# Moving the first attention's stores to ScalarE's queue, and the transposes of a feed-forward layer from TensorE to VectorE and DMA

## The chip, the cores and the metric

The kernel runs on one core of a Trainium2 chip. TensorE (PE) multiplies matrices and does transposes as a multiplication with the identity; VectorE (DVE), ScalarE (ACT) and GpSimd (POOL) work on rows; SyncE (SP) only issues DMAs here, and ACT and POOL can issue DMAs as well. Each engine works through its own instructions in order, and waits on semaphores for the others. The metric is the device time of one execution in microseconds, as a median over runs.

## The reference

A block of four layers on an input of 4 batches of 512 rows and 512 columns, in float32:

```python
x = x + attn_a(layernorm(x))   # 16 query heads, 4 key/value heads, of 128 columns
x = x + ffn(layernorm(x))      # 512 -> 1408 -> 512
x = x + attn_b(layernorm(x))   # 16 heads, weights in 4 bits with scales per block of 32
x = x + ffn(layernorm(x))      # the same weights as above
```

What the change touches is in `attn_a` and in the last `ffn`. `attn_a` is the mean of two attentions on the same projections:

```python
y     = softmax(causal(rotary(q) @ rotary(k).T * D ** -0.5)) @ v
# gated linear attention: a running state per head, with a decay per key column
S     = S * exp(logsigmoid(k) / 16) + softmax(k) outer v
o_gla = softmax(q) @ S
attn_a = (0.5 * y + 0.5 * o_gla) @ Wo
```

The feed-forward layer quantises its weights to -1, 0 and 1, and is `(sigmoid(x @ w1.T) * (x @ w2.T)) @ w3.T`.

## The kernel before

The work lies on partitions in chunks of 128 rows; a batch has 4 chunks. `bank` gives a PSUM bank. The four layers run one after another, with some preparation of each next one inside.

**First attention.** One group is a key/value head (index g) with its four query heads, on one batch (b): 16 groups, 64 chunks. `step(n)` does a piece of work for each of six neighbouring chunks, called u, v, w, x, y and z for chunks n-2 to n+3, so a chunk passes through six steps. Per chunk these pieces are:

- `A` (z): the query projection by `wq`, four query heads side by side, to `q_t`.
- `B` (z): softmax of the queries times the decay (`qd`), for the linear attention; DVE transposes it in blocks of 32 by 32 (`turned`, L461), the result is stored to DRAM (`queries`, L463, on SP, 256 KB); the rotary embedding gives `qr`, with POOL doing the products `sw` (L345).
- `L` (y, in the next step): four DMAs fetch `queries` back to `qdT` (L470), so that blocks come to stand transposed. A transpose of 128 by 128 is thus the 32 by 32 blocks by DVE and the order of the blocks by DMA.
- `C` (y): PE transposes `qr` to `qrT`.
- `D(0)` to `D(3)` (x), one for each head: scores against the group's keys up to this chunk (L490, between 128 and 512 columns), negated row maximum by DVE (L494), exponential by ACT (L497), reciprocal (DVE, L498), division by the sum on ACT (L499), transpose in blocks by DVE into `turned` (L500). After the fourth head, `D` stores `turned` as `passed` (L503, on SP, 256 KB for the first chunk of a group to 1 MB for the fourth).
- `E` (w, in the next step): four DMAs fetch `passed` back to `prT` (L509).
- `own` (w): the linear attention's scores inside the chunk (L480, from `kdT` and `qdT`), masked by DVE to `own_` (L482).
- `F` (v, a step later): POOL adds `own_` to the part of `prT` on the diagonal (L515), then PE multiplies with the state (L518) and with the values (L520), and ACT halves it into `oT` (L522).
- `G` (u): the output projection by `wo` and the residual.

`part` works on a group ahead: keys and values (`project`), `gates`, `decays` (the cumulated decays `down` and the softmax of the keys times their inverse, `kd`; the decays at the ends of three chunks are copied across partitions by three small DMAs, `ends`, L420, on SP), `transposes` and `states`. ACT issues the loads of `wq` (L386) and `wo` (L390).

`step(n)` runs for n from -7 to 65. For n from 0 to 63 PE's instructions keep the order in which they are written (`manual_schedule`). Elsewhere a scheduler orders each engine's instructions by its own estimate of times; what is wrapped in `in_place` keeps its place in the written order. The DMAs of both stores and both fetches are `in_place`. Two more jobs run inside the steps: quantising the feed-forward weights (`quant`), and the layer norm of a batch to come (`ln`).

A DMA signals its end on one of eight completion semaphores, which are dealt in turn to the DMAs of SP and ACT together; so each of these DMAs waits for the one eight issues before it.

**Feed-forward layer.** `feed_forward` loads the 22 weight blocks (`block`, L264, on SP), keeps them, and goes through the 4 batches. Per batch there are 11 blocks f: 16 matmuls (`sc`) of two weight slices with the normalised input `xn`, which is kept as two halves (`hi` rounded to a faster format, `lo` the rest), a sigmoid on ACT (L1097), the product on DVE (L1098) and its halves (`split`, L120 on ACT and L121 on DVE). Then 4 output projections of 22 matmuls, the residual (L1109) and, in the last layer, the store of the result (L1111). The halves of the next batch are made inside this loop by `halved`, in steps driven by `next(steps, None)`: DVE normalises a chunk (`xn`, L160), PE transposes it in four 128 by 128 transposes (`tp`, L165), ACT and DVE split it. The halves of batch 0 are made before the layer begins.

`project` (L188) issues the matmuls of all projections. The DMAs of the whole program: 2035 on SP, 41 on ACT, 96 on POOL.

Of the kernel before, what the change touches and what calls it, by code (L numbers as in the profile page):

```python
# [9 lines left out]
F32 = mybir.dt.float32  # L10
# [3 lines left out]
F32R = mybir.dt.float32r  # L14
AF = mybir.ActivationFunctionType
ALU = mybir.AluOpType
# [3 lines left out]
P = 128  # L20
B, S, C = 4, 512, 512
NC = S // P
NK = C // P
# [51 lines left out]
def hybrid_block(ctx: ExitStack, tc: tile.TileContext, a: dict, out: bass.AP):  # L75
# [44 lines left out]
        nc.scalar.copy(hi, src)  # L120
        engine.tensor_tensor(lo, src, hi, ALU.subtract)  # L121

    def layernorm_steps(b, sink, tag="tp", apart=False, place=lambda i: i):

        mv = lnp.tile([P, NC, 2], F32, tag="mv", name="mv")
        rstd = lnp.tile([P, NC], F32, tag="rstd", name="rstd")

        def moments(c):  # L130
            st = lnp.tile([P, 6], F32, tag="st", name="st")
            nc.vector.bn_stats(st, xs[b * NC + c])
            nc.vector.bn_aggr(mv[:, c, :], st)

        def scales(at):

            var = lnp.tile([P, NC], F32, tag="var", name="var")[:, at]
# [7 lines left out]
            nc.vector.tensor_tensor(r, r, t, ALU.mult)  # L145

        if not apart:
            for c in range(NC):
                moments(c)
                if c == 1:  # L150
                    yield
            scales(slice(0, NC))
        for c in range(NC):
            if apart:
                moments(c)
                scales(slice(c, c + 1))
            else:
                yield
            xn = lnp.tile([P, C], F32, tag="xn", name="xn", bufs=1)
            nc.vector.tensor_scalar(xn, xs[b * NC + c], mv[:, c, 0:1], rstd[:, c : c + 1], ALU.subtract, ALU.mult)  # L160
            if not apart:
                yield
            tp = bank(tag, [P, NK, P])
            for k in range(NK):
                t = nc.tensor.transpose(tp[:, k, :], xn[:, k * P : (k + 1) * P], ident)  # L165
                if k == 0:
                    place(t)
            sink(c, tp)
# [5 lines left out]
    def halved(pool, b, **kw):  # L174

        halves = [pool.tile([P, NK, S], F32R, tag=f"xn{n}", name=f"xn{n}") for n in ("hi", "lo")]
        return halves, layernorm_steps(b, lambda c, tp: split(*(h[:, :, c * P : (c + 1) * P] for h in halves), tp), **kw)

    def whole(pool, b):

# [130 lines left out]
    def first_attention_gentle(base, extra):  # L311
# [6 lines left out]
        with ExitStack() as st:  # L318
# [55 lines left out]
            class Group:  # L374
# [32 lines left out]
                def decays(self):  # L407

                    dec = bank("mm", [P, NC, D])
                    halves = [one.tile([P, NC, D], F32R, tag=tag, name=f"gate{x}") for x, tag in (("hi", "held"), ("lo", "kd"))]  # L410
                    split(*halves, self.gate)
                    project(dec.rearrange("p c d -> p (c d)"), lambda i: until, lambda i: halves[i].rearrange("p c d -> p (c d)"), 2)

                    held = one.tile([P, NC, D], F32, tag="held", name="held")
                    nc.vector.tensor_scalar(held, dec, -2.0 * GENTLE * GATE_NORM, None, ALU.max)
                    self.down = two.tile([P, NC, D], F32, tag="down", name="down")
                    nc.scalar.activation(self.down, held, AF.Exp, scale=1.0 / GATE_NORM)
                    self.ends = two.tile([P, NC - 1], F32, tag="ends", name="ends")
                    for c in range(NC - 1):
                        nc.sync.dma_start(self.ends[:, c : c + 1], self.down[P - 1 : P, c, :])  # L420
# [24 lines left out]
            class Chunk:  # L445
# [9 lines left out]
                def B(self):  # L455
                    c = self.c
                    qd = one.tile([P, HG, D], F32, tag="qd", name="qd")
                    softmax_decayed(qd, self.q_t, lambda h: self.k.down[:, c, :])

                    turned = one.tile([P, 4, HG, 32], F32, tag="turned", name="turned")  # L460
                    nc.vector.transpose(turned.rearrange("p q h t -> p h q t"), qd.rearrange("p h (q j) -> p h q j", q=4))  # L461
                    self.queries = dram.tile([P, HG * D], F32, tag="queries", name="queries", bufs=3)
                    in_place(nc.sync.dma_start(self.queries, turned.rearrange("p q h t -> p (q h t)")))  # L463
                    self.qr = two.tile([P, HG, D], F32, tag="qr", name="qr")
                    rotate(self.qr, self.q_t, turn[:, c : c + 1, 0:1, :], turn[:, c : c + 1, 1:3, :])

                def L(self):
                    qdT = two.tile([P, 4, HG, 32], F32, tag="qdT", name="qdT", bufs=4)
# [15 lines left out]
                def D(self, h):  # L484

                    c, n = self.c, self.c + 1
                    if h == 0:
                        self.turned = late.tile([P, HG * P * (3 + c % 2)], F32, tag=f"turned{c % 2}", name="turned")[:, : 4 * HG * 32 * n]
                    sc = bank("sc", [P, 4, 32 * n])
                    nc.tensor.matmul(sc.rearrange("p q (k j) -> p q k j", j=32), lhsT=self.qrT[:, h, :], rhs=self.k.krT.rearrange("p (k q j) -> p q k j", q=4, j=32)[:, :, :n, :], start=True, stop=True)  # L490
                    nm = two.tile([P, 1], F32, tag="nm", name="nm", bufs=4)
                    flat = sc.rearrange("p q x -> p (q x)")

                    nc.vector.tensor_tensor_reduce(sc, sc, causal[:, :, 32 * (3 - c) :], -1.0, 3e38, ALU.add, ALU.min, nm)  # L494
                    pr = two.tile([P, S], F32, tag="pr", name="pr", bufs=5)[:, : P * n]
# [3 lines left out]
                    nc.scalar.mul(pr, pr, den)  # L499
                    nc.vector.transpose(self.turned.rearrange("p (q h x) -> p q h x", q=4, h=HG)[:, :, h, :], pr.rearrange("p (q x) -> p q x", q=4))  # L500
                    if h == HG - 1:
                        self.passed = dram.tile([P, 4 * HG * P], F32, tag="passed", name="passed", bufs=3)[:, : 4 * HG * 32 * n]
                        in_place(nc.sync.dma_start(self.passed, self.turned))  # L503

                def E(self):
                    n = self.c + 1
# [45 lines left out]
            def step(n):  # L552
# [14 lines left out]
                    y.L()  # L567
                if n > -4:
                    next(quant, None)
                if w:  # L570
                    w.E()
                part(m, p, 0)
                if n == -6:
                    nc.scalar.dma_start(turn, a["turn"])
# [2 lines left out]
                    y.C()  # L577
                if x:
                    x.D(0)
                if z and n > -2:  # L580
                    z.A()

# [1 line left out]
                    groups[n // NC + 1].load_wq()  # L584
                if x:
                    x.D(1)
                if p:
                    next(ln, None)
                if z:
# [19 lines left out]
                    v.F()  # L609
                if x:  # L610
                    x.D(3)
                if n in (-2, *range(NC + 1, last, NC)):
                    groups[max(n // NC, 0)].load_wo()
                if p:
# [462 lines left out]
    def feed_forward(base, last, first):  # L1077

        with ExitStack() as st:
# [5 lines left out]
            ws = [block((soon, soon) if f < 2 else pools, f) for f in range(NF)]  # L1085
            xn = first
            for b in range(B):
                ready, steps = halved(base, b + 1, place=in_place) if b + 1 < B else (None, iter(()))
                hid = []
                for f, (w, _) in enumerate(ws):  # L1090
                    xs12 = []
# [7 lines left out]
                    halves = [two.tile([P, S], F32R, tag=f"h{n}", name=f"h{n}", bufs=NF) for n in ("hi", "lo")]  # L1099
                    split(*halves, hT)  # L1100
                    hid.append(halves)
                    for _ in range((f > 1) + (f == 2)):
                        next(steps, None)
                    yield b, f
                for c in range(NC):
                    y = bank("mm", [P, C])
                    project(y, lambda i: hid[i // 2][i % 2][:, c * P : (c + 1) * P], lambda i: ws[i // 2][1][:, 0, :], 2 * NF)
                    x = xs[b * NC + c]
# [85 lines left out]
```

## Time and profile before

| | us |
|---|---|
| median of 3 runs | 2468.93 (2465.59 to 2472.8) |
| profiled execution, whole | 2466.74 |
| its span | 2464.8 |
| first attention | about 0 to 1020 |
| first feed-forward layer | about 1020 to 1270 |
| second attention | about 1270 to 2210 |
| second feed-forward layer | about 2210 to 2458 |
| one group of the first attention (four steps) | 61.4 |

The time around the span is 1.94 us. Windows of the trace are in microseconds from the span's start. A row of the chain of waits has the start, the length, and the engine, operation and line of a piece of the chain that ended last. A row of the timeline has the start, the length, the engine, the line, the operation and the tiles. A row of the waits has the engine and line that waited, what it waited for, and the total, the number and the longest of the waits. SPq and ACTq are the DMA issues on these engines; PEld is the loading of weights into TensorE, which overlaps the matmuls.

### The profile page before, as it was taken

The numbers are of one execution on the slowest core, as the hardware profiler recorded it, in microseconds if no ns is written. First come the engines' busy times: TensorE is split into PE (matmuls) and PEld (weight loads), VectorE is DVE, ScalarE is ACT, GpSimd is POOL, SyncE is SP. The second block draws the span as 40 slices with busy tenths as digits, with TensorE's granted clock in tenths as the row PEclk, the third lists the DMA queues.
The fourth block names the chain that finished last, engine by engine and source line by source line (L and its number), as shares of the span: only waits on it lengthen the run. The fifth ranks groups of instructions, "written<-read, shape, count | busy, mean of one in ns | idle before, by whom it ended". The sixth has DMA issues, their size and how long they took to land.

```text
span 2464.8 us, 28979 instructions
## 1 busy us (share of the span) xinstructions
PE 2425.2 (98%) x8552; PEld 1543.2 (63%) x8552; DVE 1643.5 (67%) x3816; ACT 1210.8 (49%) x3066; POOL 387.6 (16%) x424
## 2 busy tenths in 40 slices
PE   7999999999999999899999999999999999999998
PEld 4555555555555555488876666666666666658887
DVE  5888777878788888355558676667766666663332
ACT  5666666666666665333336455444444444432221
POOL 1222222222122222022224333100000000000000
PEclk9999999999999999999999999999999999999999
DMA  4667776777656664564536777534343435333000
GB/s 137 198 191 204 201 204 182 205 205 201 180 175 192 196 180 149 193 190 129 143 125 169 199 201 200 144 105 128 91 131 87 132 92 144 78 97 121 18 18 19
DMA packets 240616, 367.11 MB, mean 149 GB/s; under 512 B 41664, under 2 KB 126912, under 8 KB 234304
## 3 DMA queue, kind: packets, MB, share of 16 engines
q1 hardware_dynamic: 214192, 305.03, 44.2%
q10 hardware_dynamic: 18576, 34.95, 4.7%
q0 software_dynamic: 7680, 25.17, 3.6%
q8 instruction: 71, 1.16, 0.2%
q14 instruction: 97, 0.79, 0.1%
HBM read 209.53 MB, written 88.34 MB: 121 GB/s over the span
## 4 chain that ended last, share of the span: by engine, by line
PE 86%; DVE 5%; DMA 3%; issue 2%; ACT 1%; SPq 1%; POOL 1%; DVEq 0%; ACTq 0%; POOLq 0%
PE mm L188 44%; PE sc L188 10%; PE sc L890 8%; PE pv L520 5%; PE sc L490 5%; PE pv L924 4%; PE tp L924 4%; PE sc L480 2%; PE tp L364 2%; PE pv L518 1%; SPq L917 1%; DMA block<-blocks 1%; PE tp L165 1%; DMA prT<-turned 1%; DMA wo<-in_Wo 0%
## 5 line engine op out<-in xcount | busy, mean ns | idle before, releaser
L895 ACT ACTIVATE pr<-sc,nm 128x512 f32<-128x512 f32 x256 | 175.9, 687 | 301.6 <-DVE nm L892 258.3
L188 PE MATMUL sc<-xnhi,block 128*128 128x512 f32 x704 | 278.6, 396 | 3.7 <-ACT hT L1097 2.8
L188 PE MATMUL sc<-xnlo,block 128*128 128x512 f32 x704 | 275.4, 391 | 0.0
L890 PE MATMUL sc<-kT,qT 128*128 128x512 f32 x512 | 262.1, 594 | 0.4 <-ACT kT L872 0.4
L188 PE MATMUL mm<-xnhi,w 128*128 128x512 f32 x512 | 254.4, 497 | 0.0
L188 PE MATMUL mm<-wo,oT 128*128 128x512 f32 x512 | 232.2, 596 | 4.4 <-DMA wo<-in_Wo 3.8
L188 PE MATMUL mm<-wq,xnT 128*128 128x512 f32 x512 | 230.9, 594 | 0.1
L892 DVE TENSOR_REDUCE nm<-sc 128x1 f32<-128x512 f32 x256 | 174.9, 683 | 73.4 <-PE sc L890 70.9
L188 PE MATMUL mm<-xnlo,w 128*128 128x512 f32 x512 | 205.8, 402 | 0.0
L912 DVE STREAM_TRANSPOSE turned<-pr 128x512 f32<-128x512 f32 x256 | 173.4, 696 | 36.8 <-ACT pr L902 34.0
L499 ACT ACTIVATE pr<-pr,den 128x128 f32<-128x128 f32 (+3 forms) x256 | 141.5, 557 | 86.3 <-DVE den L498 84.5
L902 ACT ACTIVATE pr<-pr,den 128x512 f32<-128x512 f32 x192 | 138.2, 722 | 82.3 <-DVE den L900 82.1
L345 POOL TENSOR_TENSOR sw<-q_t,turn 128x256 f32<-128x256 f32 x128 | 97.1, 780 | 495.5 <-ACT q_t L453 396.5
L490 PE MATMUL sc<-krT,qrT 128*128 128x512 f32 (+3 forms) x512 | 170.4, 434 | 0.4 <-DVE own L482 0.4
L497 ACT ACTIVATE pr<-sc,nm 128x128 f32<-128x128 f32 (+3 forms) x256 | 132.9, 520 | 64.0 <-DVE nm L494 54.9
L188 PEld LDWEIGHTS mm<-wo,oT 128*128 128x128 f32 x512 | 96.3, 191 | 105.3 <-issue 95.0
L188 PEld LDWEIGHTS mm<-wq,xnT 128*128 128x128 f32 x512 | 96.3, 191 | 105.1 <-issue 98.8
L500 DVE STREAM_TRANSPOSE turned<-pr 128x128 f32<-128x128 f32 (+3 forms) x256 | 128.4, 503 | 46.7 <-ACT pr L499 43.4
L188 PEld LDWEIGHTS sc<-xnhi,block 128*128 128x128 f32 x704 | 132.8, 189 | 33.3 <-ACT hT L1097 4.0
L188 PEld LDWEIGHTS sc<-xnlo,block 128*128 128x128 f32 x704 | 132.8, 189 | 27.8 <-issue 0.7
L520 PE MATMUL pv<-prT,v_t 128*128 128x512 f32 x320 | 148.0, 592 | 0.0
L890 PEld LDWEIGHTS sc<-kT,qT 128*128 128x128 f32 x512 | 95.8, 189 | 81.4 <-issue 63.6
(151 smaller groups left out, 4800.7 us busy)
## 6 DMA issues: line engine op xcount, KB each, us to landing
prT<-turned SPq DMA_DIRECT2D x1024, 64.0 KB, 2.0
w<-exact SPq DMA_DIRECT2D x32, 1024.0 KB, 5.5
wq<-in_Wq ACTq DMA_DIRECT2D x16, 1024.0 KB, 5.3
queries<-turned SPq DMA_DIRECT2D x64, 256.0 KB, 2.8
qdT<-queries SPq DMA_DIRECT2D x256, 64.0 KB, 3.3
wo<-in_Wo ACTq DMA_DIRECT2D x16, 1024.0 KB, 6.1
passed<-turned SPq DMA_DIRECT2D x16, 1024.0 KB, 4.3
prT<-passed SPq DMA_DIRECT2D x64, 256.0 KB, 5.9
```

Of the source, the lines that this page charges most:

```text
L188: nc.tensor.matmul(acc, lhsT=lhs(k), rhs=rhs(k), start=k == 0, stop=k == n - 1)
L490: nc.tensor.matmul(sc.rearrange("p q (k j) -> p q k j", j=32), lhsT=self.qrT[:, h, :], rhs=self.k.krT.rearrange("p (k q j) -> p q k j", q= ...
L497: nc.scalar.activation(pr, flat, AF.Exp, bias=nm, scale=-1.0, accum_out=den)
L499: nc.scalar.mul(pr, pr, den)
L500: nc.vector.transpose(self.turned.rearrange("p (q h x) -> p q h x", q=4, h=HG)[:, :, h, :], pr.rearrange("p (q x) -> p q x", q=4))
L520: nc.tensor.matmul(acc.rearrange("p h (a t) -> p h a t", a=4), lhsT=self.k.v_t[:, j, :], rhs=self.wts[:, :, :, j, :], start=j == c == 0, s ...
L890: nc.tensor.matmul(sc, lhsT=qTs[u][:, i * P : (i + 1) * P], rhs=kTs[u], start=True, stop=True)
L892: nc.vector.tensor_reduce(nm, sc, AX.X, ALU.max, negate=True)
L895: nc.scalar.activation(pr, sc, AF.Exp, bias=nm, accum_out=den)
L902: nc.scalar.mul(pr, pr, den)
L912: nc.vector.transpose(turns[u][:, :, i, :], pr.rearrange("p (q k) -> p q k", q=4))
L924: nc.tensor.matmul(accs[u].rearrange("p (n t) -> p n t", t=32), lhsT=v_ts[m, j][:, h * D : (h + 1) * D], rhs=prTs[u].rearrange("p a i (k t ...
```

## The change

**First attention.** The two stores of a chunk and the three `ends` of a group are issued by ACT instead of SP, and the first two get functions of their own with other places in `step`. `store_queries` is called at the end of the step, after `D(3)` of another chunk, where before the store followed the transpose at once. `store_rows` (the store of `passed`) is called after `D(0)` in the step after the one that computed the rows. `E`, the fetch of these rows, moves in that same step from ahead of the group's piece of work to behind `D(1)`. All these DMAs are `in_place`, the `ends` newly so.

**Second feed-forward layer.** For batches 1 to 3 `halved_by_dma` takes the place of `halved`. DVE normalises a chunk and transposes it in blocks of 32 by 32 (`to_dram`, L192 of the new kernel), SP stores the blocks to DRAM (L194, 256 KB) and fetches them back with four DMAs in transposed order (`from_dram`, L200, 64 KB each); ACT and DVE split the fetched tile into halves (`in_halves`, L205 and L206) where they split a PSUM bank before. The steps are driven once per block f and once per output projection. The first feed-forward layer and the halves of batch 0 stay as they were.

`statistics` is the first half of `layernorm_steps` under a name of its own. It changes no instruction. Lines move: L188 becomes L239, L463 L518, L503 L557, L509 L563, L515 L569, L520 L574, L420 L471, L1097 L1160.

```diff
+        def rows(c):
+            xn = lnp.tile([P, C], F32, tag="xn", name="xn", bufs=1)
+            nc.vector.tensor_scalar(xn, xs[b * NC + c], mv[:, c, 0:1], rstd[:, c : c + 1], ALU.subtract, ALU.mult)
+            return xn
...
+    def to_dram(turned, c, rows):
+        nc.vector.transpose(turned.rearrange("p q k i -> p k q i"), rows(c).rearrange("p (k q j) -> p k q j", k=NK, q=4))
+        passed = dram.tile([P, C], F32, tag="rows", name="rows", bufs=3)
+        in_place(nc.sync.dma_start(passed, turned.rearrange("p q k i -> p (q k i)")))
+        return passed
+
+    def from_dram(back, passed):
+        for q in range(4):
+            in_place(nc.sync.dma_start(back[32 * q : 32 * (q + 1)].rearrange("j (a x) -> j a x", a=4), passed.rearrange("(a j) (q x) -> q j a x", a=4, q=4)[q]))
+        return back.rearrange("p (a k i) -> p k a i", a=4, k=NK)
+
+    def in_halves(halves, c, back):
+        hi, lo = (h[:, :, c * P : (c + 1) * P].rearrange("p k (a i) -> p k a i", a=4) for h in halves)
+        in_place(nc.scalar.copy(hi, back))
+        nc.vector.tensor_tensor(lo, back, hi, ALU.subtract)
+
+    def halved_by_dma(pool, spare, b):
+        halves = [pool.tile([P, NK, S], F32R, tag=f"xn{n}", name=f"xn{n}") for n in ("hi", "lo")]
+        def steps():
+            moments, scales, rows = statistics(b)
+            for c in range(NC):
+                moments(c)
+            scales(slice(0, NC))
+            passed, backs = {}, {}
+            for c in range(NC + 2):
+                yield
+                if c < NC:
+                    passed[c] = to_dram(spare.tile([P, 4, NK, 32], F32, tag="turned", name="turned"), c, rows)
+                yield
+                if 0 < c <= NC:
+                    backs[c - 1] = from_dram(spare.tile([P, C], F32, tag="back", name="back"), passed[c - 1])
+                if c > 1:
+                    in_halves(halves, c - 2, backs[c - 2])
+        return halves, steps()
...
                     for c in range(NC - 1):
-                        nc.sync.dma_start(self.ends[:, c : c + 1], self.down[P - 1 : P, c, :])
+                        in_place(nc.scalar.dma_start(self.ends[:, c : c + 1], self.down[P - 1 : P, c, :]))
...
-                    self.queries = dram.tile([P, HG * D], F32, tag="queries", name="queries", bufs=3)
-                    in_place(nc.sync.dma_start(self.queries, turned.rearrange("p q h t -> p (q h t)")))
...
+                def store_queries(self):
+                    self.queries = dram.tile([P, HG * D], F32, tag="queries", name="queries", bufs=3)
+                    in_place(nc.scalar.dma_start(self.queries, self.blocks.rearrange("p q h t -> p (q h t)")))
...
-                    if h == HG - 1:
-                        self.passed = dram.tile([P, 4 * HG * P], F32, tag="passed", name="passed", bufs=3)[:, : 4 * HG * 32 * n]
-                        in_place(nc.sync.dma_start(self.passed, self.turned))
+
+                def store_rows(self):
+                    self.passed = dram.tile([P, 4 * HG * P], F32, tag="passed", name="passed", bufs=3)[:, : 4 * HG * 32 * (self.c + 1)]
+                    in_place(nc.scalar.dma_start(self.passed, self.turned))
...
                 if n > -4:
                     next(quant, None)
-                if w:
-                    w.E()
                 part(m, p, 0)
...
                 if x:
                     x.D(0)
+                if w:
+                    w.store_rows()
                 if z and n > -2:
                     z.A()
...
                 if x:
                     x.D(1)
+                if w:
+                    w.E()
...
                 if x:
                     x.D(3)
+                if z:
+                    z.store_queries()
...
-                ready, steps = halved(base, b + 1, place=in_place) if b + 1 < B else (None, iter(()))
+                if b + 1 == B:
+                    ready, steps = None, iter(())
+                elif last:
+                    ready, steps = halved_by_dma(base, two, b + 1)
+                else:
+                    ready, steps = halved(base, b + 1, place=in_place)
...
-                    for _ in range((f > 1) + (f == 2)):
+                    for _ in range(1 if last else (f > 1) + (f == 2)):
                         next(steps, None)
                     yield b, f
                 for c in range(NC):
+                    next(steps, None)
```

More of the change, by code (lines that the diff above doesn't have):

```diff
@@ L121, in split, with statistics @@
         engine.tensor_tensor(lo, src, hi, ALU.subtract)
-    def layernorm_steps(b, sink, tag="tp", apart=False, place=lambda i: i):
+    def statistics(b):
         mv = lnp.tile([P, NC, 2], F32, tag="mv", name="mv")
@@ L145, in scales, with layernorm_steps @@
             nc.vector.tensor_tensor(r, r, t, ALU.mult)
+        def rows(c):
+            xn = lnp.tile([P, C], F32, tag="xn", name="xn", bufs=1)
+            nc.vector.tensor_scalar(xn, xs[b * NC + c], mv[:, c, 0:1], rstd[:, c : c + 1], ALU.subtract, ALU.mult)
+            return xn
+        return moments, scales, rows
+    def layernorm_steps(b, sink, tag="tp", apart=False, place=lambda i: i):
+        moments, scales, rows = statistics(b)
         if not apart:
@@ L158, in layernorm_steps @@
                 yield
-            xn = lnp.tile([P, C], F32, tag="xn", name="xn", bufs=1)
-            nc.vector.tensor_scalar(xn, xs[b * NC + c], mv[:, c, 0:1], rstd[:, c : c + 1], ALU.subtract, ALU.mult)
+            xn = rows(c)
             if not apart:
@@ L177, in halved @@
         return halves, layernorm_steps(b, lambda c, tp: split(*(h[:, :, c * P : (c + 1) * P] for h in halves), tp), **kw)
+    def to_dram(turned, c, rows):
[14 more added lines that the diff above has]
+        def steps():
+            moments, scales, rows = statistics(b)
+            for c in range(NC):
[12 more added lines that the diff above has]
+        return halves, steps()
     def whole(pool, b):
@@ L458, in B @@
                     softmax_decayed(qd, self.q_t, lambda h: self.k.down[:, c, :])
-                    turned = one.tile([P, 4, HG, 32], F32, tag="turned", name="turned")
-                    nc.vector.transpose(turned.rearrange("p q h t -> p h q t"), qd.rearrange("p h (q j) -> p h q j", q=4))
-                    self.queries = dram.tile([P, HG * D], F32, tag="queries", name="queries", bufs=3)
-                    in_place(nc.sync.dma_start(self.queries, turned.rearrange("p q h t -> p (q h t)")))
+                    self.blocks = one.tile([P, 4, HG, 32], F32, tag="turned", name="turned")
+                    nc.vector.transpose(self.blocks.rearrange("p q h t -> p h q t"), qd.rearrange("p h (q j) -> p h q j", q=4))
                     self.qr = two.tile([P, HG, D], F32, tag="qr", name="qr")
                     rotate(self.qr, self.q_t, turn[:, c : c + 1, 0:1, :], turn[:, c : c + 1, 1:3, :])
+                def store_queries(self):
+                    self.queries = dram.tile([P, HG * D], F32, tag="queries", name="queries", bufs=3)
+                    in_place(nc.scalar.dma_start(self.queries, self.blocks.rearrange("p q h t -> p (q h t)")))
                 def L(self):
```

## The prediction

> **What bounds the kernel now.** I read the page's busy times first, then the busy times stage by stage, then the chain of waits in the second feed-forward layer, and last the queues of the loop that the change touches. The page:
>
> ```profile
> span 2464.8 us, 28979 instructions
> PE 2425.2 (98%) x8552; PEld 1543.2 (63%) x8552; DVE 1643.5 (67%) x3816; ACT 1210.8 (49%) x3066; POOL 387.6 (16%) x424
> ```
>
> TensorE (PE) is busy for all but 39.6 us. The same by stage (columns: window and its length, then busy us and instructions of PE, weight loads, DVE, ACT, POOL, then clock, DMA share, GB/s):
>
> ```profile
> 0.00:100.00 100.00, 81.71 (x286) 51.67 (x287) 68.37 (x209) 61.03 (x190) 18.11 (x28) 0.95 0.55 157
> 100.00:960.00 860.00, 859.18 (x2743) 470.02 (x2742) 693.02 (x1874) 548.24 (x1684) 188.50 (x200) 1.00 0.67 193
> 960.00:1060.00 100.00, 93.38 (x288) 53.03 (x287) 48.82 (x122) 36.27 (x92) 11.86 (x11) 0.97 0.62 198
> ...
> 2254.00:2465.00 211.00, 203.00 (x912) 167.71 (x910) 65.40 (x101) 44.66 (x76) 0.00 (x0) 0.99 0.06 21
> ```
>
> Here is the reading that decides most: in the 860 us of the steady first attention PE idles 0.82 us, at full clock. Whatever the stores and fetches there do to their queues, at most 0.8 us can be won from it. What can be won is in the ramp (18.3 us idle in the first 100), at its end (6.6 us), or by taking work off PE. It is the last that the second feed-forward layer does. Its chain of waits is PE alone:
>
> ```profile
> 2361.01 0.44 PE tp L165 x4
> 2361.45 7.31 PE sc L188 x32
> 2368.76 0.44 PE tp L165 x4
> ...
> 2398.07 38.99 PE sc L188 x172
> ```
>
> The last row is batch 3, which has no next batch to normalise: 38.99/172 = 0.2267 us a matmul. With four transposes between, 32 matmuls and the transposes repeat every 7.75 us (2361.01 to 2368.76); 32 matmuls alone are 7.25, so four transposes cost 0.48 to 0.50, with what they disturb. A batch has 264 such matmuls: 59.8 us, and 61.8 with its four sets.
>
> **The change, part by part.**
>
> *Second feed-forward layer.* Batches 1 to 3 have 4 chunks each, so 12 sets, 48 transposes, leave PE. By the period above 12 x 0.48 = 5.8 us, all on the path, since PE never stops there. The group row counts the same transposes by busy time:
>
> ```profile
> L165 PE MATMUL tp<-ident,xn 128*128 128x128 f32 x256 | 39.9, 280 | 9.7 <-DVE xn L160 9.7
> ```
>
> Its 280 ns are a latency that overlaps the next transpose; I take the period. The Trainium skill ("TensorE: Matmul & The Clock Gate", Part 4: PE-mode transpose) gives about 275 ns for one 128x128 transpose inside a kernel, close to this row's mean; by it the 48 would be worth 13.2 us. The trace's period speaks against that.
>
> What replaces them: 12 stores of 256 KB and 48 fetches of 64 KB on SP, on DVE 12 stream transposes, on ACT and DVE the split into halves from the fetched tile instead of the PSUM bank (same count, about 0.6 and 0.7 us). A DVE stream transpose of 128x512 is 0.70 us (L912, 696 ns), 8.4 us in all, in a stage where DVE is busy 65 of 211: beside PE. The one place where it is tight is batch 0. SP there issues the last 18 weight blocks from 2214.95 to 2228.84, and stores and fetches stand behind them. The last block lands about 2236.5. Four round trips follow, each one store (2.8 us by the 256 KB queries row) and a fetch (3.3 us by qdT's row), overlapped two deep: I estimate the fourth chunk back at about 2250.5. ACT takes its half just before the sigmoid of block 10, due about 2252, and the product made from that is needed at about 2257. Cover is 2 to 4 us; I cost it at 0, at most 4 us once. The two transposes that DVE does before block 0's product (2.5 us) lie under PE's wait for block loads until 2218.46: 0, at most 1. In batches 1 and 2 SP is free and the cover exceeds 20 us.
>
> *First attention: stores on ACT.* 64 query stores, 64 stores of probabilities and 48 `ends` leave SP for ACT. SP waited in front of the two stores:
>
> ```profile
> SPq L463 <- DVE turned L461: 149.3, 49, 7.3
> SPq L503 <- DVE turned L500: 131.6, 31, 7.4
> ```
>
> 280.9 us of SP waits go, and are worth nothing as PE waits for none of it. The Trainium skill ("DMA: Bandwidth & Descriptors", Issuing engines are not separate DMA queues) says that issuing from several engines saves only the sequencer's issue time; no row here shows two engines storing at once, and by the rule, too, this part gains nothing.
>
> Its cost is on ACT: 176 issues of 0.34 to 0.6 us, some 70 us, where ACT is busy 548 of 860. How an issue lies among ACT's work (the read-out between is left out):
>
> ```profile
> 547.46 0.62 ACT L233 ACTIVATE w<-w 128x512 f32<-128x512 f32 x1
> 547.93 0.37 ACTq L386 DMA_DIRECT2D wq<-in_Wq  x1
> ...
> 548.07 0.49 ACT L499 ACTIVATE pr<-pr,den 128x256 f32<-128x256 f32 x1
> ```
>
> The issue ends at 548.30 while the next ACTIVATE has run since 548.07: it is beside. Bounds: 0, or 70 us of ACT time, of which only what exceeds the slack of ACT's readers reaches PE. From the trace: finished kd to its PE transpose 4.4 us (median, least 2.65), oT to the output projection 6.4, a free score bank to its next matmul 1.4 to 3 at the tightest. One issue (0.4) is under each of these. I take 0.
>
> Waits are worse than issues. A DMA waits for the one eight issues before it, over both queues, and on ACT the exponentials stand behind it. The `ends` of one steady group, with SP's neighbours:
>
> ```profile
> 533.93 0.34 SPq L503 DMA_DIRECT2D passed<-turned  x1
> ...
> 538.47 2.03 SPq L509 DMA_DIRECT2D prT<-passed  x4
> ...
> 543.80 9.81 SPq L420 DMA_DIRECT2D ends<-down  x3
> 553.71 0.54 SPq L503 DMA_DIRECT2D passed<-turned  x1
> ```
>
> Three `ends` occupied SP for 9.81 us, and held the next store back. On ACT, `ends` two and three wait for a qdT fetch, whose own store now leaves ACT just before. From these rows (fetch about 4 us after its store, 3.3 to land) ACT would stand 1 to 1.5 us plus three issues (1.4 at most), about 2.5 us a group; kd's 4.4 covers it. 0, at most (9.8 - 4.4) x 16 groups = 86 us.
>
> *Rows fetched half a step later.* The store of probabilities now leaves after the first score block of the next chunk, the fetch after its second, behind the wq load and, on SP, two wkv issues (0.4 to 0.6 us each). Tightest is the fourth chunk of a group: above, the store left at 533.93 and the fetch at 538.47. Then POOL's addition and PE's use:
>
> ```profile
> 550.48 1.73 POOL L515 TENSOR_TENSOR prT<-prT,own 128x512 f32<-128x512 f32 x1
> ```
>
> ```profile
> 554.60 3.43 PE pv L520 x8
> ```
>
> The addition ends at 552.21, 2.4 us before PE starts, and only the last of the matmuls needs its piece. The store waited for is 1 MB and lands in 4.3 us, so the fetch could not leave before 538.3: it moves by less than 1 us. For the third chunk it moves by about 4, of 5 to 10. 0, at most 16 x 2 us.
>
> *Ramp and tail.* Two transposes of rotated queries move behind 8 matmuls, and the queues of the first chunks differ: +1, between -5 (a quarter of 18.3) and +5. The last reload of wo keeps its place on ACT; its 3.7 us wait stays.
>
> Sum: -5.8 + 0 + 0 + 1 = about -5 us. Against the profiled execution (2464.8 span, 1.94 around it, 2466.74) 2461.8. That execution is 2.2 below the runs' median of 2468.93, so the median after is put at 2464.
>
> **Rivals.**
> 1. *Slower: ACT is held by the DMA waits.* For it: the 9.81 us row, and 0.82 us of PE idle that shows no spare anywhere once readers' slack is used up. Against: kd's 4.4 us, and that most waits concern transfers issued long before. It decides when ACT stands longer than about 4.4 us per group; at 6 us, 16 x 1.6 = 26 us, less 5: 2490. Around 5.2 us, 13 - 5: 2477.
> 2. *Faster by more than the bound.* SP no longer stands behind DVE in the ramp, and about a quarter of its 18.3 us idle goes as well: -5.8 - 5, so 2458. For it: qdT's fetch is in the ramp's chain of waits (3.64 us at 61.17). Against: the rest of that chain is DVE and ACT work, which gets no shorter.
> 3. *The round trip of batch 0 is late*, by 4 us: -5.8 + 1 + 4, 2468, no change.
> 4. *The fetch is late for the fourth chunk*: 16 x 1 us, less 5: 2480.
>
> **How the numbers follow.** A measurement of this kernel tells about 0.3% from no change, 7.4 us. Forecast 0.39 (-5, with its spread -9 to -1, of which a fifth falls beyond -7.4); rival 2 0.25; rival 1 0.13; rival 3 0.16; rival 4 0.07. Faster: 0.08 + 0.25 = 0.33. Slower: rivals 1 and 4, nearly whole, 0.19. Same: 0.48. The likeliest one's own range is 2460 to 2468; with rival 2 below and part of rivals 1 and 4 above, 2455 to 2477.
>
> **What would show it.** Right: 48 fewer L165 transposes, the periods of the second feed-forward layer's batches 60 us instead of 61.8; PE idle still under 2 us from 100 to 960; the SP rows L463 and L503 gone. ACT held: PE waits for kd or gate halves, repeating every 61.4 us, and ACT waits named by its `ends` line. Late fetch: pv or POOL rows with PE behind them. Late round trip: ACT waiting for `back` near 2250, with PE idle before 2260. Any PE stall that repeats per group would make the prediction wrong, since a tenth of a microsecond per chunk is 6 us.

## The result, and the profile after

The changed kernel takes 2497.72 us (median of five runs, 2494.11 to 2501.98) where the kernel before takes 2468.93. The ratio is 1.0119, with a 95% interval of 1.0103 to 1.0135: 28.8 us, or 1.2%, slower. The forecast was 2464, in a range of 2455 to 2477.

The page of the changed kernel, profiled in an execution of 2494.11 us:

```profile
span 2492.2 us, 28872 instructions
PE 2424.0 (97%) x8504; PEld 1536.7 (62%) x8504; DVE 1631.0 (65%) x3828; ACT 1212.2 (49%) x3066; POOL 381.4 (15%) x424
```

The 48 transposes are gone (8504 for 8552), and the span is 27.4 us longer. By stage (columns as in the table of before):

```profile
0.00:100.00 100.00, 75.81 (x265) 48.29 (x266) 64.66 (x199) 56.89 (x181) 17.58 (x28) 0.95 0.50 153
100.00:960.00 860.00, 838.78 (x2667) 456.65 (x2666) 653.03 (x1813) 534.36 (x1639) 176.67 (x194) 1.00 0.65 187
960.00:1060.00 100.00, 91.18 (x249) 43.82 (x249) 63.55 (x175) 46.10 (x127) 15.87 (x16) 0.95 0.56 162
...
2254.00:2465.00 211.00, 211.00 (x934) 174.69 (x933) 85.63 (x139) 56.88 (x96) 1.01 (x1) 1.00 0.21 74
```

In the steady first attention, where PE idled 0.82 us, it now idles 21.2 of 860. That is where most of the time came from. At milestones of PE's work the changed kernel is behind by 5.5 us at its first output projection (88.15 and 93.62), by 30.3 at the decays of the last group (906.63 and 936.92), and by 37.6 at the start of the first feed-forward layer (1016.58 and 1054.19): 5.5 in the ramp, 24.8 in the steady stretch, 7.3 in the last group. From there it gains, 5.5 of it in the second feed-forward layer. The waits of PE in the changed kernel (columns: who waited for what, us in total, times, longest):

```profile
PE mm L239 <- DVE held L466: 14.4, 11, 2.1
...
PE mm L239 <- DMA wo<-in_Wo: 8.5, 2, 6.8
```

The first of these rows did not exist before. The second had 3.8 us.

**What the new wait is.** One group, on PE and DVE. First the kernel before (timeline: start, length, engine, line, operation, tiles):

```profile
535.93 0.40 PE L188 MATMUL mm<-gatelo,until 128*128 128x512 f32 x1
536.16 3.60 PE L188 MATMUL mm<-wo,oT 128*128 128x512 f32 x8
```

```profile
539.61 0.67 DVE L415 TENSOR_SCALAR held<-mm 128x512 f32<-128x512 f32 x1
```

The output projection by wo starts right behind the matmuls of the decays. DVE reads the decays 3.4 us after that start, and nobody waits for it. The changed kernel, same place:

```profile
553.02 0.39 PE L239 MATMUL mm<-gatelo,until 128*128 128x512 f32 x1
554.59 3.70 PE L239 MATMUL mm<-wo,oT 128*128 128x512 f32 x8 [1.18 <-DVE held L466]
```

```profile
553.85 0.68 DVE L466 TENSOR_SCALAR held<-mm 128x512 f32<-128x512 f32 x1
```

Now the projection waits for that read. PE's instructions stand in the same order in both, but the PSUM bank is another. `bank("mm", ...)` draws from a pool of two banks, and which one a tile gets is decided while the program is planned. In the program of the kernel before the two alternate without exception: queries' projection in one, decays in the other, output projection in the first again. In the changed program, of the 14 groups in which an output projection follows the decays, 11 give it the bank that the decays were written to just before. (The traces do not name banks; this stands in the planned programs.) It cannot write there until DVE has read it, and the trace has 11 waits for `held`, one for each.

What I take to have led the pool to it stands on ACT in that place:

```profile
551.49 0.66 ACTq L557 DMA_DIRECT2D passed<-turned  x1
552.24 0.58 ACT L504 COPY q_t<-mm 128x512 f32<-128x512 f32 x1 [1.24 <-DVE turned L553]
```

The store of the probabilities waits for DVE's last transpose, and the copy that frees the queries' bank stands behind it. In all 11 groups the store is issued less than 0.1 us after that transpose ends, and in 8 of them ACT idles for 0.6 to 1.2 us ahead of the copy. What the planner reckoned with, the trace does not tell; e4 and e5 below test it.

**The second feed-forward layer** (chain of waits, changed kernel):

```profile
2286.01 19.95 PE mm L239 x88
2305.96 39.89 PE sc L239 x176
```

A batch is 59.84 us where it was 61.77. PE has no wait in it.

### The profile page after: what moved, and what is told of

Its sections match the earlier page's. It is cut to its first block, busy times and chain, and to the rows that moved or that the text cites. A ratio compares the mean times of both kernels' runs of the same rounds, so it can differ in the third digit from the quotient of the medians.

```text
span 2492.2 us, 28872 instructions
## 1 busy us (share of the span) xinstructions
PE 2424.0 (97%) x8504; PEld 1536.7 (62%) x8504; DVE 1631.0 (65%) x3828; ACT 1212.2 (49%) x3066; POOL 381.4 (15%) x424
## 4 chain that ended last, share of the span: by engine, by line
PE 85%; DVE 5%; DMA 4%; issue 2%; ACT 1%; SPq 1%; POOL 1%; ACTq 0%; DVEq 0%; POOLq 0%
PE mm L239 43%; PE sc L239 9%; PE sc L948 9%; PE pv L574 5%; PE sc L543 5%; PE pv L982 4%; PE tp L982 4%; PE sc L533 2%; PE pv L572 2%; PE tp L415 1%; SPq L975 1%; DMA block<-blocks 1%; DMA wo<-in_Wo 1%; DVE sc L547 1%; PE tp L175 1%
## 5 line engine op out<-in xcount | busy, mean ns | idle before, releaser
L239 PE MATMUL sc<-xnhi,block 128*128 128x512 f32 x704 | 276.7, 393 | 3.6 <-ACT hT L1160 2.8
L239 PE MATMUL sc<-xnlo,block 128*128 128x512 f32 x704 | 274.2, 390 | 0.0
L239 PE MATMUL mm<-wo,oT 128*128 128x512 f32 x512 | 236.4, 605 | 23.5 <-DVE held L466 14.4
L239 PE MATMUL mm<-xnhi,w 128*128 128x512 f32 x512 | 254.4, 497 | 0.0
L239 PE MATMUL mm<-wq,xnT 128*128 128x512 f32 x512 | 230.6, 593 | 0.3 <-DVE state L493 0.3
L239 PE MATMUL mm<-xnlo,w 128*128 128x512 f32 x512 | 205.8, 402 | 0.0
L239 PEld LDWEIGHTS mm<-wo,oT 128*128 128x128 f32 x512 | 96.6, 193 | 129.6 <-issue 96.8
L239 PEld LDWEIGHTS mm<-wq,xnT 128*128 128x128 f32 x512 | 95.7, 190 | 105.1 <-issue 98.7
L239 PEld LDWEIGHTS sc<-xnhi,block 128*128 128x128 f32 x704 | 132.2, 188 | 33.2 <-ACT hT L1160 4.0
L239 PEld LDWEIGHTS sc<-xnlo,block 128*128 128x128 f32 x704 | 132.2, 188 | 27.8 <-issue 0.7
L574 PE MATMUL pv<-prT,v_t 128*128 128x512 f32 x320 | 147.8, 592 | 0.0
L569 POOL TENSOR_TENSOR prT<-prT,own 128x512 f32<-128x512 f32 x64 | 87.9, 1374 | 378.9 <-DMA prT<-passed 248.3
```

What stands on the lines that cost most here:

```text
L239: nc.tensor.matmul(acc, lhsT=lhs(k), rhs=rhs(k), start=k == 0, stop=k == n - 1)
L574: nc.tensor.matmul(acc.rearrange("p h (a t) -> p h a t", a=4), lhsT=self.k.v_t[:, j, :], rhs=self.wts[:, :, :, j, :], start=j == c == 0, s ...
```

## The experiments

"After" is the changed kernel, 2497.72.

| kernel | us | to before | idle of PE in 100 to 960 us |
|---|---|---|---|
| before | 2468.9 | | 0.8 |
| after | 2497.7 | 1.0119 | 21.2 |
| e1 feed-forward part alone | 2463.1 | 0.9964 | 1.8 |
| e2 first attention's part alone | 2503.5 | 1.0134 | 19.1 |
| e3 after, banks in turn | 2488.5 | 1.0067 | 8.6 |
| e4 after, rows stored from SP | 2476.5 | 1.0029 | 5.7 |
| e5 after, rows stored behind the copy | 2503.2 | 1.0131 | 21.8 |
| e6 e1 with ends on ACT | 2465.7 | 0.9981 | 3.3 |
| e7 e1 with rows moved, on SP | 2537.8 | 1.0280 | 49.1 |
| e8 e1 with queries on ACT | 2467.8 | 0.9990 | 5.9 |
| e9 e1 with wo reloaded first | 2461.4 | 0.9961 | 1.3 |
| e10 before, same bank | 2542.8 | 1.0286 | 47.2 |
| e11 e4 with wo reloaded first | 2471.6 | 1.0014 | 4.8 |
| e12 before, banks in turn | 2468.9 | 0.9997 | 2.7 |

The times are medians, and the differences below are between medians. The ratios are taken against the runs of before on the same chip, whose median was 2468.9 for e1 to e4, 2469.7 for e5 to e8, 2470.9 for e9 to e11 and 2468.8 for e12. They put a kernel up to 3 us from where its median does, so what differs by less than that is not told apart by times alone. The last column is 860 less the busy time of PE in that window. It differs by a microsecond between e1 and before, which have the same first attention, and there is one profile of each kernel. The ramp differs more: up to the first output projection e1 took 6.6 us longer than before, with the same instructions, mostly since ACT, and PE behind it, stood for one load of a weight slice (timeline of ACT in e1):

```profile
52.01 0.74 ACT L284 ACTIVATE w<-w 128x640 f32<-128x640 f32 x1 [6.34 <-DMA w<-in_w1T]
```

### The two parts apart: e1 and e2

e1 puts the first attention back as it was; e2 puts the second feed-forward layer back:

```diff
-                elif last:
-                    ready, steps = halved_by_dma(base, two, b + 1)
```

> The kernel before with the change of the second feed-forward layer alone; the first attention is as it was. Theory: this part keeps its price of the forecast, 12 sets of transposes at 0.48 us, and nothing is late: 5.4 to 5.8 us faster than before, about 2463.3. In the trace, the output projections of that layer start 61.8, 59.8, 59.8 and 60.2 us apart at most, and the first attention is unchanged to 0.5 us. Rival: the round trip of batch 0 takes it back: 0 to 2 us faster, about 2468.

> The kernel after with the second feed-forward layer as before; only the moves of the stores are left. Theory: the parts add up, so about 2503 (34 us slower than before, 5.5 slower than after). Rival: they interfere (other PSUM banks or queues), and the sum of e1 and e2 misses the whole by more than 3 us.

e1: 2463.14, 5.8 us faster; the ratio is 0.9964 (0.9951 to 0.9977), which is 5.7 to 12.1 us. e2: 2503.47, 34.5 slower. By the medians the sum is 28.7 and the whole 28.8, so no interference of the parts is seen. In the traces the feed-forward part's price stands clear of the ramp: from the layer's start to the last output projection, e1 is 5.8 us shorter than before (1.83, 1.93, 1.91 and 0.13 from batch to batch). All that is wrong lies in the first attention.

### The bank: e3, e10 and e12

The two banks are dealt in turn by the program instead of the pool (e3 on after, e12 on before). e10 is e12 with one line more in `decays`, after which the output projection gets the bank of the decays:

```diff
+        if tag == "mm" and ps[1][tag] == 2:
+            turns[0] += 1
+            whole = ps[0].tile([P, 512], F32, tag=f"mm{turns[0] % 2}", name=tag, bufs=1)
...
                     project(dec.rearrange("p c d -> p (c d)"), ...)
+                    turns[0] += 1
```

> The kernel after, but the two PSUM banks of the projections are dealt in strict turn, as they fell in the kernel before; stores, queues and places are as after. Bank theory: 11 of 16 groups pay 1.1 to 2.3 us since the output projection gets the bank that the decays have just been written to, and must wait until VectorE has read it; these stalls go, 16 to 20 us faster than after, 2478 to 2482. Rival (ScalarE is held by its DMA waits): the query copy out of the other bank is as late, PE waits for that instead, and at most 5 us go: above 2492.

> The kernel before with one thing of the kernel after: the output projection that follows the decays takes the same PSUM bank as they, in 15 of 16 groups; all stores at their old places. Bank theory: TensorE waits in each of them for VectorE to read the bank, 1.1 to 1.5 us and some slower clock after it: 15 to 28 us slower than before, 2484 to 2497. Rival (the stalls of after come from late engines, and the bank only shows them): less than 6 us slower, below 2475.

> The kernel before with the two banks of the projections dealt in strict turn by the program, the device by which e3 and e10 set the banks. In the steady groups the banks fall as they did before, so the theory is 2466 to 2473, no change. Rival (the device itself changes the order of the engines' work and costs): 2476 or more, and e10's price is to be taken against this run instead.

e12 is 2468.87, no change: dealing the banks by the program costs nothing by itself. e10 is 72 us slower than its before, 2542.84, far more than was expected. Its waits, and one group:

```profile
PE mm L194 <- DVE held L422: 49.2, 14, 4.7
```

```profile
574.62 0.40 PE L194 MATMUL mm<-gatelo,until 128*128 128x512 f32 x1
579.01 5.49 PE L194 MATMUL mm<-wo,oT 128*128 128x512 f32 x6 [4.00 <-DVE held L422]
```

```profile
578.29 0.67 DVE L422 TENSOR_SCALAR held<-mm 128x512 f32<-128x512 f32 x1
```

In e10 DVE reads the decays some 3 to 4 us behind, as in the kernel before. With the bank shared PE waits for it in all 14 groups in which an output projection follows the decays, for 2.5 to 4.7 us, and in 12 of them the matmuls after it run slower for a while (below). So the bank alone, on a kernel with every store at its old place, makes this wait. In the changed kernel the same wait is 0.9 to 2.1 us, as DVE reads the decays sooner there.

e3 takes the wait out of the changed kernel: no `held` row is left in 100 to 960 us, and PE's idle falls from 21.2 to 8.6. The median falls by 9.3 us, to 2488.45, less than the 16 to 20 of the bank theory and more than the 5 of its rival. What is left in that window are the two groups in which a layer norm runs beside (gate halves late) and late copies of the normalised input:

```profile
PE mm L245 <- DVE gatelo L127: 2.9, 2, 1.5
PE tp L421 <- ACT xnT L429: 2.7, 3, 1.4
PE mm L245 <- ACT gatehi L126: 1.5, 2, 0.8
```

After both late gate halves the clock was granted by half for 3.4 us, which costs another 3.4 us in all. So the bank is something over a quarter of the 34.5 us that e2 shows, and the rest has other causes.

### The store of the probabilities: e4, e5 and e7

e4 changes only who issues this store, e5 only its place on ACT:

```diff
-                    in_place(nc.scalar.dma_start(self.passed, self.turned))
+                    in_place(nc.sync.dma_start(self.passed, self.turned))
```

```diff
-                if w:
-                    w.store_rows()
                 if z and n > -2:
                     z.A()
+                if w:
+                    w.store_rows()
```

> The kernel after, but the store of the probabilities is issued by SP, at the same place in the order; the query stores and the ends stay on ScalarE. Theory: it is this store, standing on ScalarE ahead of the copy of the queries, that makes the planner give the banks otherwise; without it the banks alternate, and 16 to 22 us go: 2476 to 2482. What is left above e1 is then the ends and the query stores. Rival: the waits of the ends on ScalarE hold the group; then less than 6 us go: above 2491.

> The kernel after, but on ScalarE the store of the probabilities stands behind the projection of the next queries and its copy, instead of ahead of them; it is still ScalarE's. The planner now lets the two banks alternate. Theory (the query copy behind the waiting store is what hurts, through the bank it frees): about as e4, 2474 to 2481. Rival (a store that waits on ScalarE hurts whatever stands behind it, here the exponentials): 2486 or more.

e4: 2476.48, 21.2 us back, in the theory's range; decays and output projection have different banks again in every group. e5: 2503.22. They have different banks there too, and it is as slow as after. So it is the store ahead of the copy that goes with the shared bank, but my theory that the copy behind the store is what hurts fell. The waits of e5, and one group on ACT:

```profile
PE mm L239 <- ACT gatehi L120: 14.5, 4, 6.2
```

```profile
623.98 0.40 ACT L552 ACTIVATE pr<-pr,den 128x128 f32<-128x128 f32 x1 [3.15 <-DVE den L551]
...
625.78 0.61 ACT L120 CAST gatehi<-gate 128x512 fp32r<-128x512 f32 x1
```

In the two groups with a layer norm beside them, ACT casts the gate half 6.2 us late: the planner has put the cast behind the query exponentials, and those behind a division whose denominator DVE makes late. So it is not one place behind the store that is bad. With this store on ACT, the planner orders ACT and DVE otherwise, and something that PE needs comes late, either a bank or a gate half. That the planner's estimate of the store's wait is what moves the order is argued, not shown.

e7 moves the store and the fetch to their new places with everything on SP:

> e1 and one more edit: the store of the probabilities and its fetch at their new, later places, both on SP; queries and ends on SP as before. Theory: in the last groups SP reaches the loads of the feed-forward blocks before ScalarE issues the last reload of wo, which then lands in 8 to 9 us instead of 5.3; 4 to 6 us slower than e1, 2467 to 2469, and nothing in the steady groups. Rival (the later fetch is late for the fourth chunk of every group): 16 stalls, 2475 or more. Rival (nothing): 2463.

2537.77, 75 us slower than e1, the largest loss of an edit to e1. It is the late fetch. Its waits and one group (SP, then PE):

```profile
PE pv L575 <- DMA prT<-passed: 48.8, 10, 5.6
```

```profile
313.11 0.38 SPq L558 DMA_DIRECT2D passed<-turned  x1
318.81 2.17 SPq L564 DMA_DIRECT2D prT<-passed  x4
```

```profile
323.01 1.02 PE L573 MATMUL pv<-qdT,state 128*128 128x512 f32 x2
329.28 5.37 PE L575 MATMUL pv<-prT,v_t 128*128 128x512 f32 x8 [5.25 <-DMA prT<-passed]
```

The store stands behind the `ends` and the query fetch on SP, leaves at 313.11, is waited for by the fetch (318.81), and PE stands for 5.25 us in the fourth chunk of the group. In e4, where the query stores and `ends` have left SP, the same store and fetch at the same places cost no such wait. The moves therefore hang together: the later fetch is only possible since SP is freed, and the freed SP is paid for on ACT.

### The smaller moves: e6 and e8

Each is e1 with one of the other two moves.

```diff
-                        nc.sync.dma_start(self.ends[:, c : c + 1], self.down[P - 1 : P, c, :])
+                        in_place(nc.scalar.dma_start(self.ends[:, c : c + 1], self.down[P - 1 : P, c, :]))
```

> e1 and one more edit: the three ends of a group on ScalarE, in the written order; the stores are SP's at their old places. Theory: in the ramp the three issues (1.9 us) stand ahead of the exponential that kd needs, where nothing covers them, 2 to 4 us; in the steady groups kd's spare time covers them: 2465 to 2468. Rival (the forecast's first: ScalarE is held for longer than 4.4 us in every group): 2475 or more. Rival (no cost): within 1.5 of e1, 2463.

> e1 and one more edit: the query stores on ScalarE at the end of the step; the rest on SP as before. Theory: one issue of 0.34 us beside other work, and a wait for nothing that is not done: 2462 to 2465. Rival (the store's wait for the DMA eight issues before holds ScalarE): 2468 or more, with PE waiting for q_t or gate halves in most groups.

e6: 2465.66, 2.5 us over e1 (4 by the ratios), as expected. In the ramp PE waits 3.8 us for kd, which it hardly did in e1 (0.4). In the changed kernel the three issues stand before the exponential that kd needs, which starts at 33.48 where it started at 31.47 before, and PE waits 4.1 us for kd. The wait is 3.6 to 4.1 us in each of the seven kernels with the `ends` on ACT, and at most 2.0 in the seven others. ACT in the changed kernel, with the last two of the three issues and that exponential:

```profile
32.17 1.27 ACTq L471 DMA_DIRECT2D ends<-down  x2
33.48 0.63 ACT L473 ACTIVATE held<-held 128x512 f32<-128x512 f32 x1 [1.52 <-issue]
```

In the steady window PE idles 3.3 us, 1.5 more than in e1. e8: 2467.77, 4.6 over e1 (6 by the ratios), between the two expectations. In the steady groups PE waits for no gate half and for q_t 0.9 us in all; what it waits for more is the reload of wo (6.6 us where e1 has 3.6).

### The last reload of wo: e9 and e11

```diff
                 if u:
                     u.G()
+                if n in (-2, *range(NC + 1, last, NC)):
+                    groups[max(n // NC, 0)].load_wo()
```

> e1 and one more edit: the reload of wo is issued on ScalarE as soon as the output projection that reads the old one is written, ahead of the last score block's work, instead of behind it. Theory: the wait of 3.7 us for the last reload, and the slower clock after it, go; 2 to 5 us faster than e1: 2458 to 2461. Rival (the reload waits on ScalarE for the projection and holds the exponentials): not faster than e1, 2463 or more.

> e4 and the edit of e9. In e4 TensorE waits 6.4 us for the last reload of wo, which lands 8.5 us after its issue because SP has issued block loads ahead of it. Theory: issued some 4 us earlier, ahead of those loads, it lands in time: 4 to 8 us faster than e4, 2469 to 2473. Rival (the reload is slow for another reason than the loads ahead of it): 0 to 3 us, 2474 to 2476.

e11: 2471.63, 4.9 us faster than e4 by the medians and 3.7 by the ratios, whose intervals overlap; in the traces PE's waits for wo fall from 8.2 to 2.8 us. e9: 2461.42, 1.7 faster than e1 by the medians, but its interval (0.9948 to 0.9974) is e1's: no difference is shown. In the changed kernel the last reload is issued at 1028.22, and PE starts on it at 1036.87, 8.6 us later (before: 995.26 and 1000.65, 5.4). SP, free of its waits, had issued block loads ahead:

```profile
1025.85 2.83 SPq L315 DMA_DIRECT2D block<-blocks  x3
```

That these loads are the reason is not shown. In e9 the first block load left SP at 999.10, behind the reload, and the reload still took 8.07 us; there a fetch of probabilities (512 KB, issued from 991.73) was just ahead. What is shown is that the reload takes 5.3 us in one surrounding and about 8 in others, and that an earlier issue shortens the wait where PE stood for 6 us.

## Why the prediction was wrong

**The feed-forward layer: right.** 5.8 us from the period in the chain of waits, 5.8 in e1, by medians and in the trace. The batch period fell to 59.84 (59.8 forecast). The round trip of batch 0 was not late: ACT took the last half at 2287.37, right after the cast before it, and PE did not stop. The row's mean of 280 ns a transpose, and the skill's 275 (measured there on bf16; these are float32), would have said 13 us; the period was the right reading.

**SP's waits are worth nothing: right.** 281 us of them went, and no time was won by it. Nor was SP empty after: it waits in front of the qdT fetch, and PE for none of that:

```profile
SPq L523 <- DMA queries<-turned: 456.6, 64, 18.7
```

The rule cited in the forecast, that issuing from several engines saves only the sequencer's time, agrees with e6 and e8, which gained nothing.

**"I take 0" for the stores on ACT: this step failed.** It was worth 34.5 us. The slacks of 1.4 to 6.4 us that I set against issues and waits were read from the trace of before. They belong to one order of ACT and DVE and one dealing of the PSUM banks, and the edit made the planner choose both anew. I had compared PE's order of instructions, found it the same, and not looked at which bank each matmul writes. Of the 34.5, about 21 go with the store of the probabilities (after less e4), and some 9 of these are the bank (after less e3). On e1, the `ends` alone are 2.5 and the query stores alone 4.6. The moves depend on each other (e7), so the remaining 6 or so are not given to one of them. The trace of e4 tells where its loss lies: against e1 its stretch from the first output projection to the last decays is 3.7 us longer, the one from there to the second attention 4.8, where PE waits 8.2 us for wo instead of 3.6, and the ramp has the wait of 4.1 us for kd.

**Rival 1** gave the time to within 8 us (2490) by the wrong mechanism: ACT was not held by the waits of `ends`, which cost PE little in the steady groups (e6). Its remark that there is no spare anywhere once a reader's slack is used up was right.

**Rival 4, and "it moves by less than 1 us".** The late fetch did not happen in the changed kernel. But e7 shows that it is no small matter: 10 waits, nine of them of about 5 us, as soon as the query stores and the `ends` share SP with it. I had computed the fetch from the landing of the store and taken for granted that the store is issued in time.

**The ramp and the last reload.** +1 was forecast for the ramp; the profile has +5.5 at the first output projection. Most of it is the wait for kd that the `ends` on ACT bring (4.1 us; 2.5 in the time of e6); the rest is less than one late load made of e1's ramp. "Its 3.7 us wait stays" was wrong: 6.8.

The Trainium skill ("Perfetto Trace Analysis", Matmuls) says that independent matmul groups should rotate through different PSUM banks, so that the reading of one overlaps the matmuls of the next. e10 agrees and gives the price on this kernel: 72 us for one missed turn per group. The rule was at hand, and I did not ask whether the rotation would survive the edit.

## What to carry to other kernels

Where a planner or a pool decides orders and buffers, an edit that moves a DMA to another engine's queue is not local: compare the buffer that each instruction writes in the two programs, besides the order of the instructions, and count a pool of two as something that can be dealt the wrong way. Slack that is read from a trace holds for that trace's order only. On a kernel whose bounding engine has no idle time, as here, an edit that takes work off that engine can be priced from its period, and one that only moves queues has nothing to win and an order to lose; e1, the first without the second, is faster than both kernels.

## What the runs showed of the hardware

A wait of PE can cost more than its length. After the last reload of wo in the changed kernel (timeline of PE, then the window right after it, whose third number from the end, 0.50, is the granted clock):

```profile
1036.87 6.72 PE L239 MATMUL mm<-wo,oT 128*128 128x512 f32 x8 [6.78 <-DMA wo<-in_Wo]
```

```profile
1036.20:1040.00 3.80, 3.13 (x4) 1.50 (x5) 0.00 (x0) 0.00 (x0) 0.00 (x0) 0.50 0.38 131
```

Eight matmuls take 6.72 us where they take 3.60 in a steady group: after a wait of 6.8 us the clock is granted by half for some 6 us (0.50 from 1040 to 1043, too), and 3.1 us are lost on top of the wait. In e10, 12 of the 14 waits are followed by three to seven matmuls at half rate (0.85 us from start to start instead of 0.43). From its first output projection to the decays of the last group e10 takes 73.7 us longer than before, and 46.4 of that are idle time of PE (47.2 and 0.8 from 100 to 960); nearly all of the other 27 is the slower clock.

No length of a wait separates the two cases in these runs. All waits of 3.8 us and more in e10 (4), and the nine of 4.7 to 5.6 us in e7, are followed by a slower clock. Two in e10, of 3.37 us (before 310.00) and 3.66 us (before 716.04), are not, while two of 2.51 us are. After the changed kernel's waits of 0.9 to 1.4 us for `held` the next matmuls run at the full rate; of its two of 1.9 and 2.1 us, the shorter (before 809.90) was followed by four matmuls at half rate, the other by none. The Trainium skill ("TensorE: Matmul & The Clock Gate", HAM oscillation — how this bites in real kernels) sums its rule up as no idle gaps of TensorE over about 3.4 us; most rows here agree, but a wait of 1.9 us was enough once and one of 3.66 was not.
